# In image 0, three of sixteen units of x are loaded in 128-byte pieces and transposed by VectorE

## The chip, the cores and the metric

The kernel runs on one core of a Trainium2 chip. The metric is the device time of one execution in microseconds; "before" is the median of three runs. The engines named below are TensorE (PE; its weight loads are PEld), VectorE (DVE), ScalarE (ACT), GpSimd (POOL), and SyncE (SP), which here only issues transfers (DMAs). Transfers are carried by sixteen DMA engines.

## The reference

The input x is (4, 64, 64, 256) in float32: four images, each of N = 4096 positions with 256 channels. An attention layer is computed:

```python
q = x @ Wq + bq            # 128 channels per position
k = x @ Wk + bk            # 128 channels
v = x @ Wv + bv            # 256 channels
pq, pk, pv = (t.reshape(B, -1, N) for t in (q, k, v))
energy = einsum('bcn,bcm->bnm', pq, pk)
attention = softmax(energy, axis=-1)
out = einsum('bcm,bnm->bcn', pv, attention).reshape(B, W, H, C)
return gamma * out + x
```

The reshape is no transpose: it lays the position-by-channel block of an image out anew as channels by N. For the projections, x has to stand with its 256 channels on the partitions, so that TensorE can contract over them; in memory it lies with positions first. Somebody has to transpose it. The edit is about who.

## The kernel before

Products that need float32 accuracy are built from reduced-precision ones: a tensor y is split into forms h (upper part), l and d (combinations of y and h), and each product is taken as three matmuls over forms. ScalarE writes h, VectorE l, and d is written by VectorE or GpSimd (`split`, L153 to L168).

An image is projected in NI = 16 units of 256 positions each. Image 0 is projected first, in a loop of its own (its body begins with `products(0, i, 0, (0, 1))`), in about the first 64 us. Then comes the attention loop over 512 steps, in whose gaps the units of the next image are projected (`step`). Everything is scheduled by hand: each engine runs its instructions in the order in which the Python code issues them (`manual_schedule`), and semaphores are derived from the tiles that are written and read.

One pass of image 0's loop, for unit i, issues in this order:

- products of q and k with forms 0 and 1 of unit i (PE, L268); then `qk_forms` begins: ScalarE writes h of the tile f (L318);
- products of q and k with form 2 of unit i + 1 (PE), and then `seed_qk` (VectorE, L296), which puts the bias onto that result; the other products of unit i + 1, at the head of the next pass, accumulate onto it and so wait for it;
- VectorE's two other forms of f (L321). f holds q and k of unit i in all three forms and is stored to DRAM. Tiles f rotate over three buffers (two of the tag `pf`, and `f3`), so the L318 of unit i + 3 overwrites what unit i's stores read;
- products of v for unit i (PE); ScalarE's and VectorE's forms of v (L156, L159), GpSimd's third (L162); products of v with form 2 of unit i + 1, and `seed_v` (ScalarE, L303);
- `transposed(0, i + 3)`: four TensorE transposes of 128 x 128 into a PSUM tile `xt` (L230); then `x_forms(0, i + 3)`: ScalarE (L156), VectorE (L159), GpSimd (L162) split `xt` into the forms of x;
- `load_x(0, i + 6)`: SP loads a unit of x, 256 KB, into one of four slots `xs4` (L207). Each slot is read by the transposes of the unit before in it;
- `store()`: the stores of f, two of q and two of k for each unit, issued by SP (L349; for the units 0 to 3 one of them goes over GpSimd, L347);
- in the passes 7 to 14, parts of the first two attention steps (`cross` L379 and L380, `energy` L394 and L397, `upper` L403), and now and then a load of k by GpSimd (L366).

So SP's order in image 0 is: load of unit i + 6, stores of unit i, load of unit i + 7, stores of unit i + 1, and so on. Each of SP's transfers signals one of eight semaphores in turn, so that a ninth one waits until the first has landed.

For the images 1 to 3 the transpose is made in another way. There x is loaded by SP in eight transfers for a unit (L755), each of 32 KB in pieces of 128 bytes, so that every 32-channel group comes to lie on its own quarter of the partitions; a transpose of 32 x 32 blocks by VectorE (one instruction of 128 x 512, L226) then gives the same `xt` as TensorE's four transposes.

Of the kernel before, what the change touches and what calls it, by code (L numbers as in the profile page):

```python
# [20 lines left out]
def kernel(  # L21
# [36 lines left out]
    nc = tc.nc  # L58
# [5 lines left out]
    KC = C // P  # L64
# [5 lines left out]
    def columns(t, nb):  # L70
        return t.rearrange("b w h c -> b (w h c)").rearrange(
            "b (a s g f) -> b g a s f", a=P, s=2, f=nb
        )

    XB = 256
    xv = columns(x, XB)
# [24 lines left out]
    with ExitStack() as fast:  # L101
# [45 lines left out]
        active, stores, xloads = [], [], []  # L147
# [41 lines left out]
        def bank(name, shape, b, ring):  # L189
            if b:  # L190
                tile_ = spare(name, shape)
                now["turn"] += 1
                return tile_
            pool, tag = next(rings[ring])
            return pool.tile(shape, F32, tag=tag, name=name)

        def spare(name, shape):
            pool, tag = now["banks"][now["turn"] % len(now["banks"])]
            return pool.tile(shape, F32, tag=tag, name=name)

        def load_x(b, i):
            if b == B or i >= NI:
                return
            if b == 0:
                t = xs4[:, i % 4]
                if i:
                    nc.sync.dma_start(t, xv[b, i])  # L207
                loads["x", b, i] = t
                return
            pair = work.tile([P, 2, 2, XB], F32, tag="xd", name=f"x_{b}_{i}", bufs=1)  # L210
            for u in range(2):
                raw_x = pair[:, u].rearrange("p s f -> p (s f)")
                for q in range(4):
                    for k in range(KC):
                        to = raw_x[q * 32 : (q + 1) * 32, k * XB : (k + 1) * XB]
                        pieces = xv[b, i + u].rearrange(
                            "(c j) s (k q i) -> q k j s c i", j=32, k=KC, q=4
                        )
                        xloads.append((to.rearrange("j (s c i) -> j s c i", s=2, c=4), pieces[q, k]))
                loads["x", b, i + u] = raw_x  # L220

        def transposed(b, i):
            xs = loads.pop(("x", b, i))
            tp = units["xt", b, i] = bank(f"xt_{b}_{i}", [P, KC, 2, P], b, 0)
            if b:
                nc.vector.transpose(tp.rearrange("p k s a -> p (k s a)"), xs)  # L226
                return
            for k in range(KC):
                for s in range(2):
                    nc.tensor.transpose(tp[:, k, s, :], xs[:, s, k * P : (k + 1) * P], ident)  # L230
# [333 lines left out]
        def step(n, engine):  # L564
# [25 lines left out]
            elif engine == "act":  # L590
                if r in (3, 4):
                    begin(("x", r - 3), x_forms(b, i + r - 3))
                elif r in (7, 8):
                    begin(("qk", r - 7), qk_forms(b, i + r - 7))
                elif r in (10, 12):
                    seed_v_pair(b, i, r // 12)
                    if r == 12:
                        load_x(b + (i + 2) // NI, (i + 2) % NI)
                elif r in (11, 13):
                    begin(("v", r // 13), v_pair_forms(b, i, r // 13))  # L600
            else:
                if r in (1, 2):
                    transposed(b, i + r - 1)
                elif r in (3, 4):
                    next(made["x", r - 3])
                    next(made["x", r - 3])
                elif r == 5:
                    seed_qk(b, i)
                    seed_qk(b, i + 1)
                elif 7 <= r <= 10:  # L610
                    next(made["qk", (r - 7) // 2])
                    if r % 2 == 0:
                        next(made["qk", (r - 7) // 2], None)
                elif 11 <= r <= 14:
                    next(made["v", (r - 11) // 2])
                    if r % 2 == 0:
                        next(made["v", (r - 11) // 2], None)
# [7 lines left out]
        for i in range(4):  # L625
            load_x(0, i)
        transposed(0, 0)
        warm(2)
        w0, w1, x0 = weights(0), weights(1), x_forms(0, 0)
# [9 lines left out]
        products(0, 0, 0, (2,))  # L639
        seed_qk(0, 0)  # L640
        transposed(0, 1)
        warm(1)
        load_x(0, 4)
        x1 = x_forms(0, 1)
        next(x1)
# [54 lines left out]
        for n in range(B * STEPS):  # L700
            b, u = divmod(n, STEPS)
            g, t = divmod(u, NU)
# [13 lines left out]
            p = n - 2 + (n > 17)  # L716
# [32 lines left out]
            for m in range(2 * NU):  # L749
                c, r = divmod(n + NU - 3 - 13 * m // 16, STEPS)  # L750
# [11 lines left out]
    with tc.If(nc.values_load(again[0:1, 0:1]) > 0), ExitStack() as general:  # L762
# [91 lines left out]
        for b in range(B):  # L854
# [16 lines left out]
            for g in range(NG):  # L871
                ps = []
                mx = work.tile([P, 2, NB], F32, tag="mx", name=f"gmx_{b}_{g}")
                for t in range(NP):
# [9 lines left out]
                    p = ppool.tile([P, 2, NB], F32, tag="p", name=f"gp_{b}_{g}_{t}")  # L884
# [89 lines left out]
```

## Time and profile before

| | us |
|---|---|
| median of three runs | 2299.38 (2299.34 to 2299.46) |
| profiled execution | 2299.69 |
| its span in the trace | 2297.9 |
| TensorE busy | 2286.7 (100%) |
| VectorE busy | 2160.7 (94%) |
| ScalarE busy | 1794.1 (78%) |
| GpSimd busy | 445.0 (19%) |

Times in the views are microseconds from the start of the span. A row of a timeline has the start, the duration, the engine, the line, the operation with its tiles, the count of merged instructions, and in brackets the engine's idle time before it with what ended it. "SPq" marks an instruction by which SP issues a transfer; its duration is the issue, not the transfer. A row of a table by stretches has the stretch, its length, the busy time of PE, PEld, DVE, ACT and POOL (instructions in brackets), TensorE's granted clock as a share of full speed, the busy share of the DMA engines and GB/s. A row of a DMA queue has its packets, megabytes and the share of the sixteen engines' time. The names `qv`, `xf`, `xt`, `f` and `v` in the rows are the tiles named above.

### The profile page before, as it was taken

Reading aid. Unit: us, or ns where it says so; the run is one execution under the profiler, and the core shown is the slowest. Engines: PE = TensorE matmul, PEld = TensorE weight load, DVE = VectorE, ACT = ScalarE, POOL = GpSimd, SP = SyncE. Lnnn points to the kernel's source line nnn. Section 1 sums busy time; section 2 is a strip of 40 time slices with the busy share of each in tenths; the row PEclk is TensorE's granted clock in tenths of the full one; section 3 lists DMA queues with packets and bytes.
Section 4 is the critical chain, followed back from the end, with each engine's and each line's share of the span. In section 5 each row is a group of like instructions: output and inputs, shape, how many; then the busy total and the mean of one; then the engine's idle time right before and its main releaser. Section 6 shows DMA issues by size and latency. Waiting matters only on the chain.

```text
span 2297.9 us, 31904 instructions
## 1 busy us (share of the span) xinstructions
PE 2286.7 (100%) x10566; PEld 1911.9 (83%) x10566; DVE 2160.7 (94%) x2222; ACT 1794.1 (78%) x2917; POOL 445.0 (19%) x747
## 2 busy tenths in 40 slices
PE   9999999999999999999999999999999999999998
PEld 9888888888888888888888888888888888888886
DVE  8999999999999999999999999999999899888888
ACT  7778777787777877777777778777788777888885
POOL 7111111111231111111122111111112211111110
PEclk9999999999999999999999999999999999999999
DMA  8567766677996777666799667766689855555554
GB/s 272 161 171 212 196 179 165 174 211 194 279 278 195 195 195 193 178 170 183 208 293 287 179 178 207 199 177 170 169 227 300 243 149 144 135 137 147 151 142 107
DMA packets 305743, 445.31 MB, mean 194 GB/s; under 512 B 129698, under 2 KB 183204, under 8 KB 305572
## 3 DMA queue, kind: packets, MB, share of 16 engines
q0 software_dynamic: 105584, 296.79, 49.6%
q1 hardware_dynamic: 199568, 146.14, 20.8%
q8 instruction: 87, 1.43, 0.3%
q14 instruction: 84, 0.69, 0.1%
q10 hardware_dynamic: 420, 0.26, 0.0%
HBM read 313.79 MB, written 112.26 MB: 185 GB/s over the span
## 4 chain that ended last, share of the span: by engine, by line
PE 99%; DVE 0%; ACT 0%; DMA 0%; issue 0%; SPq 0%; DVEq 0%
PE a L453 40%; PE e L394 20%; PE b L453 20%; PE e L379 10%; PE qv L268 5%; PE v L285 3%; PE xt L230 0%; DMA xs<-in_x_dram 0%; ACT qv L303 0%; DVE ld L431 0%; PE zp L526 0%; DVE o_last L556 0%; DVE o_last L551 0%; DVE qv L296 0%; DVE o_last L557 0%
## 5 line engine op out<-in xcount | busy, mean ns | idle before, releaser
L397 ACT ACTIVATE x<-e 128x512 f32<-128x512 f32 x960 | 522.0, 596 | 324.1 <-PE e L394 324.1
L380 ACT ACTIVATE e<-e 128x512 f32<-128x512 f32 x1024 | 546.3, 571 | 114.9 <-PE e L379 114.9
L453 PE MATMUL a<-h,v 128*128 128x512 f32 x2048 | 631.3, 389 | 0.0
L453 PE MATMUL b<-ld,v 128*128 128x512 f32 x2048 | 631.0, 389 | 0.1
L453 PE MATMUL a<-ld,v 128*128 128x512 f32 x2048 | 630.9, 389 | 0.0
L414 DVE TENSOR_TENSOR s<-s,x 128x1024 f32<-128x1024 f32 x480 | 584.1, 1217 | 48.2 <-ACT x L397 46.7
L366 POOL DMA_DIRECT2D k<-kf x512 | 273.0, 533 | 1799.9 <-PE e L394 1750.0
L429 DVE TENSOR_TENSOR ld<-x,h 128x1024 fp32r<-128x1024 f32 x480 | 584.6, 1218 | 22.6 <-ACT h L403 22.2
L431 DVE SCALAR_TENSOR_TENSOR ld<-h,x 128x1024 fp32r<-128x1024 f32 x480 | 584.5, 1218 | 0.0
L394 PE MATMUL e<-q,k 128*128 128x512 f32 x2048 | 547.6, 389 | 0.0
L403 ACT ACTIVATE h<-x 128x1024 fp32r<-128x1024 f32 x480 | 510.7, 1064 | 14.2
L453 PEld LDWEIGHTS b<-ld,v 128*128 128x128 f32 x2048 | 384.1, 188 | 80.9 <-DVE ld L431 1.1
L453 PEld LDWEIGHTS a<-ld,v 128*128 128x128 f32 x2048 | 384.4, 188 | 80.4
L394 PEld LDWEIGHTS e<-q,k 128*128 128x128 f32 x2048 | 384.2, 188 | 79.8
L453 PEld LDWEIGHTS a<-h,v 128*128 128x128 f32 x2048 | 381.3, 188 | 76.0
L379 PE MATMUL e<-q,k 128*128 128x512 f32 x1024 | 315.4, 389 | 0.0
L379 PEld LDWEIGHTS e<-q,k 128*128 128x128 f32 x1024 | 192.0, 188 | 39.9
L321 DVE SCALAR_TENSOR_TENSOR f<-f,qv 128x512 fp32r<-128x512 f32 x128 | 85.7, 680 | 0.3
L268 PE MATMUL qv<-wf,xf 128*128 128x256 f32 x576 | 77.2, 285 | 0.5 <-DVE qv L296 0.2
L268 PEld LDWEIGHTS qv<-wf,xf 128*128 128x128 f32 x576 | 73.7, 191 | 3.7 <-DVE xf L166 0.6
L429 DVE TENSOR_TENSOR ld<-s,h 128x1024 fp32r<-128x1024 f32 x32 | 39.2, 1227 | 37.0 <-ACT h L403 34.3
L166 DVE SCALAR_TENSOR_TENSOR vf<-vf,v 128x512 fp32r<-128x512 f32 x96 | 65.3, 681 | 0.0
(87 smaller groups left out, 1098.5 us busy)
## 6 DMA issues: line engine op xcount, KB each, us to landing
k<-kf POOLq DMA_DIRECT2D x512, 384.0 KB, 3.8
vf<-vf SPq DMA_DIRECT2D x96, 384.0 KB, 4.8
v<-vf POOLq DMA_DIRECT2D x96, 384.0 KB, 6.1
kf<-f SPq DMA_DIRECT2D x128, 192.0 KB, 3.9
qd<-f SPq DMA_DIRECT2D x124, 192.0 KB, 4.0
q<-qd POOLq DMA_DIRECT2D x31, 768.0 KB, 4.9
o<-o POOLq DMA_DIRECT2D x31, 512.0 KB, 5.4
o<-in_x_dram POOLq DMA_DIRECT2D x31, 512.0 KB, 6.8
```

The source lines that it names most:

```text
L268: nc.tensor.matmul(to[:, s, :], left, right.rearrange("p s a -> p (s a)") if w else right, start=(f == 2 and s == k == 0), stop=(f == 1 an ...
L321: nc.vector.scalar_tensor_tensor(f[:, :, :, j, :], h.bitcast(F32), s, y, ALU.mult, op)
L366: nc.gpsimd.dma_start(t, kf[b, u % NU])
L379: nc.tensor.matmul(e, *forms(n, i, 2), start=True, stop=False, skip_group_check=True)
L380: nc.scalar.mul(e, e, -REST)
L394: nc.tensor.matmul(e, *forms(n, i, f), start=False, stop=(f == 1), skip_group_check=True)
L397: nc.scalar.activation(x[:, i, :], e, AF.Exp, scale=(1.0 + E) ** 3 / E)
L403: nc.scalar.activation(h, units[n], AF.Identity, scale=UPPER)
L414: nc.vector.tensor_tensor(s, s, x, ALU.add)
L429: nc.vector.tensor_tensor(l, x, h.bitcast(F32), ALU.subtract)
L431: nc.vector.scalar_tensor_tensor(d, h.bitcast(F32), 1.0 + E, x, ALU.mult, ALU.subtract)
L453: nc.tensor.matmul(to, vall[:, t, i, f, j * P : (j + 1) * P], units[n][f][:, i, :], start=(t == 0 and i == 0 and f != 1), stop=(t == NU - ...
```

## The change

For image 0, the units 8, 11 and 14 get what all units of the later images have: eight transfers in 128-byte pieces, issued by SP in the place of one, and one VectorE transpose in the place of four TensorE transposes. The other thirteen units stay as they were. The pieces' addresses move into a function of their own, which the later images use too, unchanged in what it does. The tile `xt`, its PSUM bank and all that reads it stay.

```diff
+        def x_pieces(t, b, i):
+            pieces = xv[b, i].rearrange("(c j) s (k q i) -> q k j s c i", j=32, k=KC, q=4)
+            for q in range(4):
+                for k in range(KC):
+                    to = t[q * 32 : (q + 1) * 32, k * XB : (k + 1) * XB]
+                    yield to.rearrange("j (s c i) -> j s c i", s=2, c=4), pieces[q, k]
+
+        BLOCKS = (8, 11, 14)
+
         def load_x(b, i):
             if b == B or i >= NI:
                 return
             if b == 0:
                 t = xs4[:, i % 4]
-                if i:
+                if i in BLOCKS:
+                    t = t.rearrange("p s f -> p (s f)")
+                    for to, pieces in x_pieces(t, b, i):
+                        nc.sync.dma_start(to, pieces)
+                elif i:
                     nc.sync.dma_start(t, xv[b, i])
                 loads["x", b, i] = t
                 return
...
             for u in range(2):
                 raw_x = pair[:, u].rearrange("p s f -> p (s f)")
...
+                xloads.extend(x_pieces(raw_x, b, i + u))
                 loads["x", b, i + u] = raw_x
 
         def transposed(b, i):
             xs = loads.pop(("x", b, i))
             tp = units["xt", b, i] = bank(f"xt_{b}_{i}", [P, KC, 2, P], b, 0)
-            if b:
+            if b or i in BLOCKS:
                 nc.vector.transpose(tp.rearrange("p k s a -> p (k s a)"), xs)
                 return
```

More of the change, by code (lines that the diff above doesn't have):

```diff
@@ L212, in load_x @@
                 raw_x = pair[:, u].rearrange("p s f -> p (s f)")
[L213 to L219, printed above, removed]
+                xloads.extend(x_pieces(raw_x, b, i + u))
                 loads["x", b, i + u] = raw_x
```

## The prediction

> **What bounds the kernel now.** I read the page first: engine shares, then the chain of work that ended last.
>
> ```profile
> span 2297.9 us, 31904 instructions
> PE 2286.7 (100%) x10566; PEld 1911.9 (83%) x10566; DVE 2160.7 (94%) x2222; ACT 1794.1 (78%) x2917; POOL 445.0 (19%) x747
> PE 99%; DVE 0%; ACT 0%; DMA 0%; issue 0%; SPq 0%; DVEq 0%
> ```
>
> TensorE is busy nearly throughout and holds 99% of the chain. So time taken from PE is won only if nothing else becomes late, and a microsecond of PE stall in image 0 is a microsecond at the end. The edit lies in image 0's projection stage (up to about 64 us), so I read three stretches there: each engine's busy time, the granted clock, the DMA share and GB/s.
>
> ```profile
> 25.30:28.60 3.30, 3.30 (x31) 3.30 (x30) 3.07 (x6) 2.44 (x5) 3.30 (x5) 1.00 0.96 311
> 32.00:35.30 3.30, 3.30 (x30) 3.30 (x29) 3.07 (x7) 2.44 (x5) 2.53 (x3) 1.00 1.08 379
> 46.20:49.50 3.30, 3.30 (x29) 3.22 (x28) 3.16 (x6) 3.27 (x7) 2.60 (x4) 1.00 0.67 236
> ```
>
> PE fills every 3.3 us; VectorE has 0.23 us free of 3.30, and the DMA engines are full until some time after 35 us. The clock is full, so it plays no part. Three resources have little to spare: PE, VectorE, and SP's queue with the DMA engines behind it.
>
> **TensorE: what is removed.** The timeline of PE at the transposes of units 8 and 9:
>
> ```profile
> 29.66 0.60 PE L230 MATMUL xt<-ident,xs 128*128 128x128 f32 x4
> 30.01 1.68 PE L268 MATMUL qv<-wf,xf 128*128 128x256 f32 x12
> 32.97 0.60 PE L230 MATMUL xt<-ident,xs 128*128 128x128 f32 x4
> 33.33 0.84 PE L268 MATMUL qv<-wf,xf 128*128 128x256 f32 x5
> ```
>
> Four transposes hold the next matmuls back by 30.01 - 29.66 = 0.35 us. Three units: -1.05 us, the most that can be won.
>
> **VectorE: what is added.** The same transpose runs for the later images. Its group, VectorE at units 8, 11 and 14, and the first product that needs the last seed:
>
> ```profile
> L226 DVE STREAM_TRANSPOSE xt<-x x48: 715/720/722, 82.2 to 1712.0; 128x512 f32<-128x512 f32 x48
> 30.43 0.68 DVE L159 SCALAR_TENSOR_TENSOR v<-v,qv 128x512 fp32r<-128x512 f32 x1
> 31.35 0.69 DVE L159 SCALAR_TENSOR_TENSOR xf<-xf,xt 128x512 fp32r<-128x512 f32 x1 [0.23 <-ACT xf L156]
> 31.95 0.69 DVE L296 SCALAR_TENSOR_TENSOR qv<-qv,bias 128x512 f32<-128x512 f32 x1
> ...
> 39.46 1.28 DVE L321 SCALAR_TENSOR_TENSOR f<-f,qv 128x512 fp32r<-128x512 f32 x2
> 40.66 0.68 DVE L159 SCALAR_TENSOR_TENSOR v<-v,qv 128x512 fp32r<-128x512 f32 x1
> 43.06 0.70 DVE L296 SCALAR_TENSOR_TENSOR qv<-qv,bias 128x512 f32<-128x512 f32 x1 [0.62 <-PE qv L268]
> ...
> 54.39 0.70 DVE L296 SCALAR_TENSOR_TENSOR qv<-qv,bias 128x512 f32<-128x512 f32 x1 [0.62 <-PE qv L268]
> ```
>
> ```profile
> 30.72 0.59 ACT L156 ACTIVATE xf<-xt 128x512 fp32r<-128x512 f32 x1
> 38.82 0.61 ACT L318 ACTIVATE f<-qv 128x512 fp32r<-128x512 f32 x1
> 50.14 0.61 ACT L318 ACTIVATE f<-qv 128x512 fp32r<-128x512 f32 x1
> ```
>
> ```profile
> 44.65 1.68 PE L268 MATMUL qv<-wf,xf 128*128 128x256 f32 x12
> 55.98 1.68 PE L268 MATMUL qv<-wf,xf 128*128 128x256 f32 x12
> ```
>
> The price is not only 0.72 us of VectorE: ScalarE's first form of x (0.59) must wait for the transpose, VectorE's form waits for ScalarE's, and behind that in VectorE's order stands the next seed (L296), which PE's next products need. Unit 8: the v form ends at 30.43 + 0.68 = 31.11; transpose to 31.83; ScalarE to 32.46 with 0.04 of hand-over (0.04 as in 30.72 + 0.59 to 31.35); VectorE's form from there, the seed 0.60 later (31.35 to 31.95), done at 33.75. PE without the four transposes wants it at 33.33 - 0.35 = 32.98 and restarts about 33.80: instead of winning 0.35 it is 0.47 later than before.
>
> At units 11 and 14 an energy step lies between, and VectorE waits 0.62 us for PE ahead of the seeds at 43.06 and 54.39. The same chain there gives a seed at 44.0 against PE's demand at 44.65 + 0.47 - 0.35 = 44.77: hidden, and the 0.35 won. By the engines alone the edit is 0.47 - 0.35 - 0.35 = -0.2 us.
>
> **SP's queue: what is added and moved past.** One 256 KB load becomes eight of 32 KB, three times; 21 more issues. Behind them on SP, in order, stand the stores of q and k and the next loads. SP's timeline, with image 1's sixteen such pieces for the price:
>
> ```profile
> 18.70 0.63 SPq L207 DMA_DIRECT2D xs<-in_x_dram  x1
> 20.64 0.80 SPq L349 DMA_DIRECT2D kf<-f  x2
> 22.03 0.57 SPq L207 DMA_DIRECT2D xs<-in_x_dram  x1
> 29.33 0.55 SPq L207 DMA_DIRECT2D xs<-in_x_dram  x1
> 30.57 0.32 SPq L349 DMA_DIRECT2D kf<-f  x1
> 32.06 0.68 SPq L349 DMA_DIRECT2D qd<-f  x1
> 33.89 0.52 SPq L349 DMA_DIRECT2D kf<-f  x1
> 36.06 0.55 SPq L207 DMA_DIRECT2D xs<-in_x_dram  x1
> 39.21 0.74 SPq L207 DMA_DIRECT2D xs<-in_x_dram  x1
> 68.20 10.55 SPq L755 DMA_DIRECT2D x<-in_x_dram  x16
> ```
>
> Sixteen pieces in 10.55 us is 0.66 each, so a unit holds SP for 5.28 us. Three stores hold it 1.4 us (20.64 to 22.03; so units 0 to 3), four 2.1 (33.89 to 36.06), the last issued 1.5 behind the first (30.57 to 32.06), a whole load 0.6. Played forward without a gap, since every store's data is ready earlier than its turn: unit 8's pieces 18.70 to 23.98; stores of unit 2 to 25.4, load 9 to 26.0, stores 3 to 27.5, load 10 to 28.1, stores 4 to 30.2; unit 11's pieces to 35.46; stores 5 from 35.46 (before: 30.57), the last issued at 36.96, SP free at 37.6; loads and stores of two more iterations to 42.96; unit 14's pieces to 48.24; the last of stores 8 at 49.74.
>
> Who waits: f has three buffers, so ScalarE's L318 for unit u+3 waits until the stores of unit u have landed. Unit 8's L318 is at 38.82, unit 11's at 50.14. From issue to landing the stores (L349) took, at about 21 and at about 31 us:
>
> ```profile
> DMA to landing us min/median/max: 2.1/2.7/2.7
> DMA to landing us min/median/max: 4.7/4.8/4.9
> ```
>
> I take 4.0, between the ends but nearer the loaded one, because the DMA engines are only partly drained while SP issues small pieces. Stores 5 land at 40.96; PE stands 0.47 later, so ScalarE wanted to write at 39.29 and is 1.7 late. From 40.96: ScalarE to 41.57, two f forms from 41.6 (1.20), v form to 43.48, transpose of unit 11 to 44.20, ScalarE and VectorE as above, seed done at 46.12 against 44.77: a stall of 1.35. PE then stands 0.47 - 0.35 + 1.35 = 1.47 late. Stores 8 land at 53.74; the write was wanted at 50.14 + 1.47 = 51.61; the same chain ends with the seed at 58.94 against 55.98 - 0.35 + 1.47 = 57.10: 1.84 of stall. The other units' stores come in time (unit 9's last issue at 52.4 lands at 56.4, wanted at 53.91 + 2.96).
>
> The sum: 0.47 - 0.35 + 1.35 - 0.35 + 1.84 = +2.96 us. With landings of 2.7 it is +1.7, with 5.0 it is +4.0.
>
> Costed at nothing: the landing of the pieces (unit 8's last issue by 24, first read at 31; unit 14's by 48.3, read after 56; cover gone only if SP is some 7 us later still); loads 12, 13 and 15, which have as much room; ScalarE's longer wait at the transpose, part of the chain above; after image 0 the work is the same, a later start moves it as a whole, and SP has drained its queue before image 1's pieces at 68.20.
>
> **The DMA engines.** The queue's share for the stretch of image 1's pieces (70 to 79 us) and for a stretch of mostly 1 KB packets (16 to 18.6 us):
>
> ```profile
> q1 hardware_dynamic: 3543, 0.43, 32.6%
> q1 hardware_dynamic: 533, 0.62, 73.4%
> ```
>
> 0.326 x 9 x 16 us over 3543 is 13 ns a packet, and 0.734 x 2.6 x 16 over 533 is 57 ns. A unit in pieces (2048 packets) takes 1.7 us of the sixteen engines, whole (256) 0.9. Since SP needs 5.28 us to issue it, the engines have time; added to the sum: nothing.
>
> The Trainium skill (DMA: Bandwidth & Descriptors, the opening table) holds that line rate needs at least 512 B, with a read-modify-write below. Then a piece would cost a 512 B packet, about half of 57 ns; the 13 ns here speak against it. What the sum would be by it is rival 3.
>
> **Against the measure.** The profiled run took 2299.69 us, 1.8 more than its span and 0.3 more than the median of 2299.38. The sum is a difference within that run and is put on the median: 2299.4 + 3.0 = 2302.4 us. A difference under 0.2% (4.6 us) is no change here.
>
> **Rivals.**
> 1. SP's lateness is covered after all (landings of 2.7 us and quicker issues): only the engine terms stay, -0.2, at best -1.05, at worst +0.8, 2298.3 to 2300.2. For it: the stores landed that fast at 20 us. Against: the 5.28 us of issue alone are more than an iteration.
> 2. Slower by over 0.2%: pieces issue slower than 0.66 us under a full DMA load. Every 0.01 us adds 24 x 0.01 = 0.24 us at stores 8, so from 0.73 it decides; at 0.80 the sum is +6.3, 2305.7 us. For it: the group of image 1's pieces reaches 2085 ns, and whole loads reach 737 at the time of full DMA; against: its median.
>
> ```profile
> L755 SPq DMA_DIRECT2D x<-in_x_dram x384: 578/611/2085, 68.2 to 1695.5; - x192
> L207 SPq DMA_DIRECT2D xs<-in_x_dram x5: 546/546/737, 29.3 to 43.4; - x5
> ```
>
> 3. A 128 B packet holds a DMA engine as long as half a 1 KB packet, 28 ns and not 13: 2048 x 28 / 16 is 3.6 us a unit, 1.9 more, and if both late stores land so much later, the sum is 3.0 + 3.8 = +6.8, 2306.2 us. Against it: the 13 ns counted above. The rule cited above would lead here.
> 4. The whole image stage is quicker and wins over 0.2%: PE's terms cannot give 4.6 us.
>
> **How the numbers follow.** Forecast (+1.2 to +4.4, that is 2300.6 to 2303.8): 0.64. Rival 1: 0.12. Rival 2: 0.21. Rival 3: 0.02. Rival 4: 0.01. Under 0.2% either way lie the forecast and rival 1: 0.76; slower: 0.23; faster: 0.01. The range leaves out half of rival 1 below and the far part of rivals 2 and 3 above: 2299.2 to 2305.8.
>
> **What would show it.** Right: SP issuing pieces at 0.66 us without a gap; stores of units 5 and 8 starting near 35.5 and 48.2; ScalarE idle before L318's successor at units 8 and 11, its releaser a DMA; PE idle before the products near 45 and 57, about 3 us in all, and image 0 ending some 3 us later. Wrong: L318 never waiting for a DMA (rival 1), a pitch above 0.73 (rival 2), a full DMA share while pieces flow (rival 3), or a difference that arises after 64 us.

## The result and the profile after

The changed kernel takes 2308.23 us (median of 6 runs, 2306.87 to 2311.72) beside 2299.47 us for the kernel before in the same comparison (6 runs, 2299.34 to 2301.96): a ratio of 1.004, 95% interval 1.0029 to 1.005. It is slower, by about 8.8 us. The prediction was +3.0 us. The profiled execution took 2307.9 us, 8.2 us more than that of the kernel before, and the readings below explain those 8.2 us. Every line number from L207 on is 7 to 13 higher than before: L325 is the write of `f` that was L318, L328 the two VectorE forms of `f` (L321), L356 the stores (L349), L275 the projections' products (L268).

The page of the kernel after: span, engines, and the chain of work that ended last.

```profile
span 2306.1 us, 31912 instructions
PE 2288.5 (99%) x10554; PEld 1912.8 (83%) x10554; DVE 2162.7 (94%) x2225; ACT 1794.4 (78%) x2917; POOL 445.3 (19%) x747
PE 98%; DMA 1%; ACT 0%; DVE 0%; SPq 0%; issue 0%; ACTq 0%; DVEq 0%
```

Twelve matmuls are gone and three VectorE transposes have come, as planned. What is new is "DMA 1%", where it was 0%: the chain now runs through transfers, on stores that land. SP's timeline after (start, duration of the issue, line, count) shows why:

```profile
18.71 5.36 SPq L218 DMA_DIRECT2D xs<-in_x_dram  x8
...
27.59 0.47 SPq L356 DMA_DIRECT2D qd<-f  x1
...
28.86 0.56 SPq L356 DMA_DIRECT2D kf<-f  x1
...
31.39 0.84 SPq L356 DMA_DIRECT2D qd<-f  x1
32.33 5.86 SPq L218 DMA_DIRECT2D xs<-in_x_dram  x8
38.30 0.54 SPq L356 DMA_DIRECT2D kf<-f  x1
...
39.85 0.47 SPq L356 DMA_DIRECT2D qd<-f  x1
...
46.95 5.29 SPq L218 DMA_DIRECT2D xs<-in_x_dram  x8
```

The eight pieces hold SP for 5.36, 5.86 and 5.29 us (0.67, 0.73 and 0.66 us each), and every store stands behind them: the stores of unit 5 begin at 38.30, where before they began at 30.57. It is the issuing that holds SP, and not the turn of the eight semaphores: between 18.71 and 58.0 us SP issues 59 transfers with 4.6 us between them in all, the two longest gaps being 0.54 and 0.44 us, and its waits for a landing sum to 0.9 us from 16 to 72 us. Who waits, in ScalarE's timeline (the bracket is the engine's idle time before the row and what ended it; the rows are the writes of `f` for units 6, 7 and 8):

```profile
33.71 0.60 ACT L325 ACTIVATE f<-qv 128x512 fp32r<-128x512 f32 x1 [1.61 <-DMA qd<-f]
...
37.18 0.60 ACT L325 ACTIVATE f<-qv 128x512 fp32r<-128x512 f32 x1 [1.04 <-DMA qd<-f]
...
45.04 0.60 ACT L325 ACTIVATE f<-qv 128x512 fp32r<-128x512 f32 x1 [4.46 <-DMA qd<-f]
```

Three writes of `f` wait for the stores that read the buffer three units ago. Unit 11's write, at 57.28, does not. The landing times of the transfers issued in three stretches, the stores of unit 4 (28.5 to 32 us), of unit 5 (38 to 40.2) and of unit 8 (52 to 55):

```profile
DMA to landing us min/median/max: 5.7/6.2/6.8
DMA to landing us min/median/max: 2.2/5.0/5.1
DMA to landing us min/median/max: 2.0/2.0/2.8
```

TensorE's timeline after, and behind it the row of the kernel before that answers to the last one:

```profile
33.49 1.21 PE L275 MATMUL qv<-wf,xf 128*128 128x256 f32 x8 [0.41 <-DVE qv L303]
35.78 0.71 PE L275 MATMUL qv<-wf,xf 128*128 128x256 f32 x4 [1.07 <-DVE f L328]
36.33 1.60 PE L275 MATMUL qv<-xf,wf 128*128 128x256 f32 x12
37.77 0.60 PE L237 MATMUL xt<-ident,xs 128*128 128x128 f32 x4
...
47.10 1.20 PE L275 MATMUL qv<-wf,xf 128*128 128x256 f32 x4 [3.51 <-DVE f L328]
48.09 2.76 PE L275 MATMUL qv<-xf,wf 128*128 128x256 f32 x12
50.65 1.06 PE L237 MATMUL xt<-ident,xs 128*128 128x128 f32 x4
...
53.31 1.60 PE L275 MATMUL qv<-xf,wf 128*128 128x256 f32 x12
...
64.67 0.72 PE L275 MATMUL qv<-wf,xf 128*128 128x256 f32 x4 [0.79 <-DVE f L328]
...
67.93 0.71 PE L275 MATMUL qv<-wf,xf 128*128 128x256 f32 x4 [0.15 <-DVE f L328]
...
72.17 0.63 PE L386 MATMUL e<-q,k 128*128 128x512 f32 x2
```

```profile
64.42 0.63 PE L379 MATMUL e<-q,k 128*128 128x512 f32 x2
```

The first energy step behind image 0's projections starts 72.17 - 64.42 = 7.75 us later, nearly all of the 8.2; what follows costs no more than it did. Two things make it up. First, PE stands still: 0.41 + 1.07 + 3.51 + 0.79 + 0.15 = 5.93 us. Second, behind the longest stop the same instructions take longer: twelve matmuls 2.76 us where the row at 36.33 has 1.60, four transposes 1.06 instead of 0.60. The stretches say why (PE, PEld, DVE, ACT and POOL busy with counts, granted TensorE clock, DMA share, GB/s):

```profile
22.00:25.30 3.30, 3.30 (x31) 3.30 (x30) 3.07 (x6) 2.44 (x5) 3.06 (x4) 1.00 0.63 128
35.30:38.60 3.30, 2.82 (x22) 2.81 (x23) 2.96 (x6) 2.26 (x5) 2.29 (x2) 1.00 0.43 78
42.40:46.20 3.80, 1.19 (x10) 0.94 (x8) 0.53 (x1) 1.16 (x3) 0.00 (x0) 0.91 1.05 379
46.20:49.50 3.30, 2.40 (x11) 2.43 (x12) 2.58 (x5) 1.93 (x5) 1.28 (x1) 0.50 0.95 325
49.50:53.00 3.50, 3.50 (x21) 3.50 (x20) 3.15 (x6) 3.41 (x7) 1.94 (x2) 0.59 0.36 59
```

The granted clock falls to 0.50. From the restart at 47.10 to 53.31 PE runs four matmuls, twelve, four transposes and twelve matmuls, in 6.21 us. At full speed these take, by the starts of rows, 0.55 (35.78 to 36.33), 1.44 (36.33 to 37.77), 0.35 (the transposes of before, 29.66 to 30.01) and 1.44 again, 3.78 in all: the lower clock costs 2.4 us. Not all of it is the clock's alone. The twelve behind the transposes need a seed that VectorE finished at 50.20 (it began at 49.51 and took 0.69), so by an estimate from these rows PE at full clock would have reached them at 49.44 and stood for some 0.8 us. So 5.9 of stops, 2.4 of half clock, less 1.05 for the transposes that PE no longer does, is 7.3; image 0 had to account for 8.1, since its first rows ran 0.34 earlier than before (the transposes of unit 4 at 16.07 and 16.41). The other 0.8 us lies in how a row counts idle time. It counts from the end of the last matmul, which is shown 0.28 us long, while in a dense row the next one starts 0.12 us behind it. Counted from start to start, the five stops cost 6.7 us and not 5.9, and 6.7 + 2.4 - 1.05 is 8.1.

The last two columns hold the third reading. While SP issues pieces the DMA engines are half empty (0.63 and 0.43, at 128 and 78 GB/s); behind them, when the held-back stores and loads come out together, they are full (1.05). This full stretch is where the stores of unit 5 land.

### The profile page after: what moved, and what is told of

The parts are those of the page before. It is cut to its first block, busy times and chain, and to the rows that moved or that the text cites. A ratio compares the mean times of both kernels' runs of the same rounds, so it can differ in the third digit from the quotient of the medians.

```text
span 2306.1 us, 31912 instructions
## 1 busy us (share of the span) xinstructions
PE 2288.5 (99%) x10554; PEld 1912.8 (83%) x10554; DVE 2162.7 (94%) x2225; ACT 1794.4 (78%) x2917; POOL 445.3 (19%) x747
## 4 chain that ended last, share of the span: by engine, by line
PE 98%; DMA 1%; ACT 0%; DVE 0%; SPq 0%; issue 0%; ACTq 0%; DVEq 0%
PE a L460 40%; PE b L460 20%; PE e L401 20%; PE e L386 10%; PE qv L275 4%; PE v L292 3%; DMA qd<-f 1%; SPq L356 0%; PE xt L237 0%; ACT qv L310 0%; ACT f L325 0%; DVE f L328 0%; ACT v L156 0%; DVE ld L438 0%; ACT h L410 0%
## 5 line engine op out<-in xcount | busy, mean ns | idle before, releaser
L328 DVE SCALAR_TENSOR_TENSOR f<-f,qv 128x512 fp32r<-128x512 f32 x128 | 85.7, 680 | 7.0 <-ACT f L325 6.5
L275 PE MATMUL qv<-wf,xf 128*128 128x256 f32 x576 | 79.0, 287 | 6.4 <-DVE f L328 5.5
L275 PEld LDWEIGHTS qv<-wf,xf 128*128 128x128 f32 x576 | 74.9, 193 | 10.5 <-issue 6.1
```

Of the source, the lines that this page charges most:

```text
L275: nc.tensor.matmul(to[:, s, :], left, right.rearrange("p s a -> p (s a)") if w else right, start=(f == 2 and s == k == 0), stop=(f == 1 an ...
L328: nc.vector.scalar_tensor_tensor(f[:, :, :, j, :], h.bitcast(F32), s, y, ALU.mult, op)
```

## Experiments

The theory after this reading, called S: what costs the time is the number of issues on SP, eight in the place of one; they hold back the stores, `f` becomes free late, and PE stops. Against it stand the new VectorE work, the 128-byte packets themselves, the buffers of `f` being too few, and the lower clock as a cost of its own. All edits are shown against the changed kernel unless said otherwise; each ratio is to the kernel before, in the same comparison. The ratios are those on record with their intervals; they are not the quotients of the two medians and differ from them by up to 0.05%.

**The VectorE transposes alone.** Units 8, 11 and 14 are loaded whole.

```diff
-                if i in BLOCKS:
-                    t = t.rearrange("p s f -> p (s f)")
-                    for to, pieces in x_pieces(t, b, i):
-                        nc.sync.dma_start(to, pieces)
-                elif i:
+                if i:
                     nc.sync.dma_start(t, xv[b, i])
```

> The three units are loaded whole as before, and VectorE transposes them; the 32 x 32 blocks stand in the wrong places, with all the work done. Theory (late stores behind the pieces): the loss is gone, -0.5 to +0.8 us against before, no wait of ScalarE's first form of f for a DMA; PE waits once, at unit 8's seed, by some 0.5 us. Rival (VectorE's chain): +4 us or more.

Measured: 2300.37 us beside 2299.61, +0.8 us, ratio 1.0003 (0.9994 to 1.0013). No write of `f` waits for a transfer. TensorE's timeline of this kernel:

```profile
33.57 1.99 PE L273 MATMUL qv<-wf,xf 128*128 128x256 f32 x12 [0.41 <-DVE qv L301]
```

The stop of 0.41 us at unit 8's seed is the only one above 0.2 us here, and the same that stands in the changed kernel at 33.49. The VectorE side is worth about what the interval can resolve. Even by the far ends of both intervals (6.7 us for the changed kernel, 3.0 here) 3.7 us come from the loads.

**The pieces alone.** The loads in pieces stay, TensorE transposes all sixteen units (the units' layout is then not that of the reference).

```diff
-            if b or i in BLOCKS:
+            if b:
```

> Units 8, 11 and 14 are loaded in pieces, but PE transposes them with its four transposes as before; the three units' channels stand in the wrong order, with all the work done. Theory (late stores behind the pieces): the whole loss of the changed kernel stays, +6.5 to +10 us against before. Rival (pieces cost only together with VectorE's transposes): within 2 us of before.

Measured: 2309.41 beside 2299.58, +9.8 us, ratio 1.004 (1.0025 to 1.0054). The waits of this kernel:

```profile
ACT f L324 <- DMA qd<-f: 11.6, 4, 4.9
```

The loads alone lose the whole time, as expected.

**Eight transfers without small packets.** The same three units in eight transfers each, but of sixteen partitions, so with rows of 1 KB: 32 packets a transfer in the place of 256 of 128 bytes. TensorE transposes them.

```diff
-                    t = t.rearrange("p s f -> p (s f)")
-                    for to, pieces in x_pieces(t, b, i):
-                        nc.sync.dma_start(to, pieces)
+                    for q in range(8):
+                        rows_ = slice(q * 16, (q + 1) * 16)
+                        nc.sync.dma_start(t[rows_], xv[b, i][rows_])
...
-            if b or i in BLOCKS:
+            if b:
```

> The kernel before, with the loads of units 8, 11 and 14 cut into eight transfers of 16 partitions with rows of 1 KB: as many issues of SP as in the changed kernel, but no 128-byte packets and PE's transposes. Theory A (it is the number of issues that holds SP: 21 more): SP's pitch is 0.5 us or more for these too, and the loss is +3 to +9 us. Theory B (the 128-byte packets hold the DMA engines or make each issue long): the pitch is 0.4 or less or the stores are soon through again, and the loss is under +2 us.

Measured: 2309.32 beside 2299.58, +9.7 us, ratio 1.0041 (1.0027 to 1.0055). SP's timeline, the waits and one stretch of this kernel:

```profile
19.20 5.12 SPq L218 DMA_DIRECT2D xs<-in_x_dram  x8
...
32.70 6.18 SPq L218 DMA_DIRECT2D xs<-in_x_dram  x8
...
47.40 5.78 SPq L218 DMA_DIRECT2D xs<-in_x_dram  x8
```

```profile
ACT f L325 <- DMA qd<-f: 11.7, 4, 3.9
```

```profile
35.30:38.90 3.60, 3.20 (x25) 3.14 (x26) 2.57 (x5) 1.87 (x5) 2.67 (x3) 1.00 0.22 64
```

This is the run that decides. With an eighth of the packets an issue holds SP as long (0.64, 0.77 and 0.72 us each), the wait for stores is as long as with pieces alone (11.7 and 11.6 us), and so is the loss, as far as intervals of some 3 us either way can tell. The packets' size is not the cause; with 1 KB rows the DMA engines are even emptier while the pieces are issued (0.22). What costs is the number of issues.

**More buffers for f.** The writes of `f` of units 3, 4, 5, 9 and 10 go to parts of `v`'s tile that are not yet written, so that fewer of them wait for a store.

```diff
+            if b == 0 and (3 <= i <= 5 or 9 <= i <= 10):
+                f = vall[:, NU - 1 - i % 3].rearrange("p s f (w a) -> p (s f w a)", w=2)
+                f = f.rearrange("p (s w f a) -> p s w f a", s=2, w=2, f=3)
-            if b == 0 and i % 3 == 2:
+            elif b == 0 and i % 3 == 2:
```

> The changed kernel, with the tiles f of units 3, 4, 5, 9 and 10 placed in slots of v that are not yet written, so that a store has about six passes of time and not three. Theory (the wait is for the f buffer): ScalarE's first form of f waits for no DMA, the stall of 3.5 us of PE and the clock drop behind it go, and the time is 0 to +3 us against before; what may be late next are the whole loads of x behind the pieces (unit 12's). Rival (the DMA engines as such are too busy, whichever buffer is used): +6 us or more.

Measured: 2309.05 beside 2299.61, +9.4 us, ratio 1.0036 (1.0022 to 1.005). I had overlooked that units 8 and 11 still share a buffer. Unit 8's wait is gone; the one write of `f` that waits for a store is unit 11's, by 5.7 us, and it stops PE instead. TensorE's timeline of this kernel:

```profile
59.32 0.87 PE L275 MATMUL qv<-wf,xf 128*128 128x256 f32 x4 [4.58 <-DVE f L331]
```

So a second version gives each late unit a buffer that no earlier unit holds (units 3 to 5 and 9, 10 in five parts of `v`, the rest in turn):

```diff
+            if b == 0 and i in (3, 4, 5, 9, 10):
+                f = vall[:, NU - 6 + i if i < 6 else NU - 11 + i].rearrange("p s f (w a) -> p (s f w a)", w=2)
+                f = f.rearrange("p (s w f a) -> p s w f a", s=2, w=2, f=3)
-            if b == 0 and i % 3 == 2:
+            elif b == 0 and i in (2, 8, 13):
```

> The changed kernel with f tiles of five units in slots of v not yet written, so arranged that a store has four to six passes of time up to unit 13 (in the run six_f units 8 and 11 still shared a buffer). Theory (the loss is ScalarE's wait for the stores of f): no such wait over 1 us, no clock drop, and +0.8 (VectorE's chain) to +3 us against before; what is left would be PE's wait for the late whole loads of x behind the pieces. Rival (SP and the DMA engines are short of time in sum, and what waits is only a matter of place): +5 us or more, with the wait at PE's transposes, at loads of k or at later stores.

Measured: 2307.09 beside 2299.58, +7.5 us, ratio 1.0031 (1.002 to 1.0041). The theory is missed, the rival met. The waits, TensorE's timeline and a stretch of this kernel:

```profile
ACT f L328 <- DMA qd<-f: 6.1, 2, 4.1
```

```profile
59.26 0.64 PE L237 MATMUL xt<-ident,xs 128*128 128x128 f32 x4 [1.86 <-issue]
...
69.78 1.22 PE L275 MATMUL qv<-xf,wf 128*128 128x256 f32 x8 [3.18 <-ACT qv L310]
```

```profile
69.70:71.00 1.30, 1.22 (x9) 1.22 (x10) 1.30 (x3) 0.03 (x1) 0.00 (x0) 1.00 1.07 392
```

The stops for `f` in the middle are gone, and two others have come. At 59.26 PE has stood 1.86 us ahead of transposes; the profile names no releaser, but the whole load that SP issued at 56.01, behind unit 14's pieces and unit 8's stores, landed at 59.16. And PE stands 3.18 us before 69.78, at a seed of ScalarE that comes behind a late write of `f`: at the end of image 0 a write has waited 4.1 us for a store again. (In this execution image 0 also began 1.7 us later than in that of the changed kernel: unit 8's first piece is issued at 20.43 and not 18.71.) SP issues from 20.43 us to the end of image 0 almost without a gap. From the load of unit 8 on, the kernel before issues 56 transfers that hold SP 28.8 us out of 45.9; with 21 more it is 77 that hold it 43.7 us in the changed kernel and 43.9 here, nearly all of the 45.9 that this part took before. SP has no slack left to work lateness off. More buffers move the place where this is paid; they do not pay it.

**The pieces spread out.** On the same buffers, the pieces are issued three, three and two behind the stores of three passes (shown against that version).

```diff
+        later = []
...
-                    for to, pieces in x_pieces(t, b, i):
-                        nc.sync.dma_start(to, pieces)
+                    later.extend(x_pieces(t, b, i))
...
+            for to, pieces in later[:3]:
+                nc.sync.dma_start(to, pieces)
+            del later[:3]
```

> As deep_f, but the pieces of a unit are issued 3, 3 and 2 in three passes, behind each pass's stores, in the place of eight in a row ahead of them. Theory: no load or store of x or f is later than its slack, +0.5 to +1.5 us against before. Rival (SP and the DMA engines are short in sum): no better than deep_f, +4 us or more.

Measured: 2314.41 beside 2299.58, +14.8 us, ratio 1.0061 (1.0044 to 1.0078). The waits of this kernel:

```profile
DVE xt L233 <- DMA xs<-in_x_dram: 12.1, 3, 6.2
```

Now the stores go first and the x tiles themselves come too late: VectorE waits 12.1 us for them. That is the rival's case: spreading takes nothing from the sum on SP.

**The pieces off SP.** The pieces are issued by ScalarE and GpSimd, two each in two passes.

```diff
+        later = []
...
-                    for to, pieces in x_pieces(t, b, i):
-                        nc.sync.dma_start(to, pieces)
+                    later.extend(x_pieces(t, b, i))
...
+            for m, (to, pieces) in enumerate(later[:4]):
+                (nc.scalar, nc.gpsimd)[m % 2].dma_start(to, pieces)
+            del later[:4]
```

> The changed kernel, with the 24 pieces issued by ScalarE and GpSimd (two each in the passes u - 6 and u - 5 of a unit u, behind what they do in the pass) and none by SP. The DMA engines carry the same 128-byte packets. Theory (SP's time to issue is what is short): the stores of f are in time, no wait of ScalarE's first form for them, and the time is +0.5 to +3 us against before (VectorE's chain, and what the issues take of ScalarE and GpSimd). Rival (the packets on the DMA engines): +5 us or more with waits for stores as in the changed kernel.

Measured: 2307.41 beside 2299.51, +7.9 us, ratio 1.0032 (1.002 to 1.0044). The expectation is missed. The waits of this kernel, and from the timelines of GpSimd and of ScalarE's issues:

```profile
PEld qv L275 <- POOL xf L162: 2.7, 3, 1.9
...
DVE xt L233 <- DMA xs<-in_x_dram: 2.5, 1, 2.5
...
ACT s L404 <- DMA kf<-f: 2.0, 1, 2.0
...
ACT f L325 <- DMA kf<-f: 1.2, 1, 1.2
```

```profile
24.14 1.29 POOL L696 DMA_DIRECT2D xs<-in_x_dram  x2
```

```profile
47.13 2.52 ACTq L696 DMA_DIRECT2D xs<-in_x_dram  x2
```

What S says of `f` holds: of 7.1 us of waiting for stores 1.2 are left. But the issues cost elsewhere. One takes about 0.65 us on GpSimd (1.29 for two), and GpSimd writes forms of x that PE needs; PE's weight loads wait for it three times. VectorE waits 2.5 us for a piece. And the longest stop of PE, 2.44 us before 52.74, leads back to ScalarE: of the 2.52 us in the last row two issues take 0.59 each, and in between ScalarE stands until a store of k that SP had issued has landed (the 2.0 us in the waits), for its transfers and SP's signal the same eight semaphores in turn; behind this its write of `f` comes at 50.67. The run moves the cost and doesn't take it away, so it does not separate the issues from their queue. With units 11 and 14 alone handled so (unit 8 as before):

> As off_sp, with the units 11 and 14 alone, whose VectorE chain was worked out to be hidden. If both chains are hidden and the issues find room on ScalarE and GpSimd, PE gains 2 x 0.35 us: -0.7 to 0 against before. If the issues delay ScalarE's or GpSimd's forms: 0 to +2.

2305.63 beside 2299.51, +6.1 us, ratio 1.0024 (1.0014 to 1.0034): missed as well. Its longest stop is 2.10 us before 48.34, again at `f`'s forms.

**One unit at a time.** `BLOCKS` is cut to unit 8, and to unit 14.

```diff
-        BLOCKS = (8, 11, 14)
+        BLOCKS = (8,)
```

> The changed kernel with unit 8 alone in pieces. Theory (SP's issues pile up from unit to unit and the piled-up lateness meets the f buffers): the lateness of one unit is worked off in three passes, the time is +0.5 to +2.5 us against before, and the three units cost more together than three times one. Rival (each unit has its own price): +2.5 to +3.5.

Measured: 2303.46 (2300.91 to 2306.8) beside 2299.51, +4.0 us by the medians and 3.0 by the ratio, 1.0013 (1.0004 to 1.0023); more than expected. The profiled execution was the longest of the ten, 2306.8 us; image 0 began late in it, unit 8's first piece being issued at 20.98 and not 18.71, that is, ahead of the first transfer that the edit touches. TensorE's timeline and a stretch of it:

```profile
38.53 1.19 PE L275 MATMUL qv<-wf,xf 128*128 128x256 f32 x4 [2.09 <-DVE f L328]
```

```profile
38.50:41.00 2.50, 2.47 (x11) 2.50 (x12) 2.35 (x5) 0.99 (x2) 1.94 (x2) 0.50 0.94 321
```

A stop of 2.09 us, and then half clock. The late write of `f` ahead of this stop waited for the stores of unit 3, which stood behind the pieces: the profile names a product of PE as its releaser, but the last of these stores, issued at 29.83, landed 6.5 us later, at 36.36, and the write began at 36.47. Whether such a stop halves the clock, and how late image 0 begins, may be what spreads these ten runs over 5.9 us, where those of before lie within 2.5; only one of them has a trace, so this is not shown.

> The changed kernel with unit 14 alone in pieces. Theory (piled-up lateness): -0.35 to +2 us against before; the stores of unit 8 land about 1 us late for unit 11's first form. Rival (each unit has its own price): +2.5 to +3.5.

Unit 14 alone: 2300.8 (2299.38 to 2304.09) beside 2299.51, +1.3 us, ratio 1.0005 (0.9996 to 1.0014). Its longest stop is at unit 11's `f`, by the stores of unit 8 behind the pieces; one of 0.58 us at the seed follows (57.97). TensorE's timeline:

```profile
54.80 0.71 PE L275 MATMUL qv<-wf,xf 128*128 128x256 f32 x4 [1.63 <-DVE f L328]
```

That is where the prediction had put a stall of 1.84 us, in a kernel without the other two units. That the sizes are so near is in part luck: the prediction had PE 1.47 us late by then, and here one of unit 8's stores held SP 1.92 us. Nor do the two runs show lateness piling up: three times 4.0 would be more than the 8.8 of three units, and unit 14's interval (-0.9 to +3.2 us) reaches into the rival's range. With the buffers of the second version above:

> Unit 14 alone in pieces, with the f tiles of deep_f, so that the stores of unit 8, late behind the pieces, hold nobody in unit 11. Theory (late stores are the price, VectorE's chain at unit 14 is hidden): the stall of 1.6 us of the run only_14 goes, and PE wins its four transposes, -0.4 to +0.4 us against before. Rival (SP's lateness only moves, to the loads or the later stores): +1 us or more, as only_14.

2299.94 beside 2299.46, +0.5 us, ratio 1.0000 (0.9991 to 1.001). No write of `f` waits for a store, and TensorE's timeline has the first energy step behind the projections where it stood before (64.42):

```profile
64.39 0.63 PE L389 MATMUL e<-q,k 128*128 128x512 f32 x2
```

One unit's seven extra issues were hidden by more buffers, three units' were not. Nothing is won either; no version was faster than the kernel before.

**The clock.** Does the half clock cost its 2.4 us beside the stop? In the longest stop, the pass of unit 9, PE gets 28 matmuls with weights of zero that add nothing to a bank.

```diff
+            if i == 5:
+                zero_r = vall[:, NU - 1, 0, 0, :P]
+                nc.gpsimd.tensor_scalar(zero_r, ones, 0.0, None, ALU.mult)
+            if i == 9:
+                for m in range(28):
+                    nc.tensor.matmul(
+                        units[0, 0, 9][:, m % 2, :], zero_r, wf[:, 0, 0, 0],
+                        start=False, stop=(m > 25), skip_group_check=True,
+                    )
```

> The changed kernel, with 28 products of zero weights (about 3.3 us) added to the sums of unit 9 at the place where PE stood idle for 3.5 us; they add nothing to the result. If the granted clock of 0.5 from 47 to 52 us comes from that idle time, it stays at full and the time is 2 to 3 us less than the changed kernel's, about +6 against before. Rival (the clock falls for another cause, or what PE loses at half clock is hidden behind VectorE and ScalarE): the same as the changed kernel or slower, +8 to +12.

Measured: 2308.82 beside 2299.61, +9.2 us, ratio 1.0039 (1.0024 to 1.0053). A stretch, and TensorE's timeline:

```profile
44.00:48.00 4.00, 4.00 (x36) 4.00 (x35) 2.52 (x4) 2.49 (x6) 1.26 (x1) 1.00 1.07 395
```

```profile
43.39 3.52 PE L666 MATMUL qv<-wf,v 128*128 128x256 f32 x28
...
61.33 0.98 PE L275 MATMUL qv<-wf,xf 128*128 128x256 f32 x3 [2.60 <-DVE f L328]
```

With PE busy the clock stays at 1.00 in the place where it had fallen to 0.50: the idle stretch is what lowers it. But the time does not come back. PE comes earlier to the pass of unit 12, and there stands 2.60 us for unit 11's `f`, which in the changed kernel came in time. The same fill at unit 12 as well:

> As filled_gap, with 28 products of zero weights also in the pass of unit 12, where PE stood idle for 2.6 us in that run and the granted clock fell behind it. Theory C (the half clock after an idle stretch of PE adds its own time to the stall): no stretch at half clock in image 0, and 2 to 3 us less than the changed kernel, about +6 against before. Theory S (SP's issues set the pace of the stage; PE at full clock only comes earlier to the next wait): the clock stays full, and the time is within 1.5 us of the changed kernel's, +7.5 to +10 against before.

2309.4 beside 2299.46, +9.9 us, ratio 1.0044 (1.0028 to 1.0059), with the clock full in all of image 0; but here the second fill itself holds PE some 3 us. That is in theory S's range. What the half clock costs by itself stays open. What is shown is that PE's pace was not the limit: taking the 2.4 us away let PE run into the next late store.

## Why the prediction was wrong

Its mechanism was right in kind: SP's issues hold back the stores, `f` becomes free late, and PE stops. The sum gave +3.0, the runs +8.8. It forecast 4.0 us of stops (0.82, 1.35 and 1.84) less 1.05; image 0 shows 6.7 us of stops less 1.05, and 2.4 us of half clock. The steps that failed are SP's time to issue under load, the landing time, the two units whose stores were not tested, and the clock.

- **TensorE, -1.05 us.** Twelve matmuls went, and nothing speaks against 0.35 us a unit; it can't be seen by itself in the end time.
- **VectorE's chain.** Right: PE at unit 8's seed was forecast to restart 0.47 us late, at 33.80; measured 33.49 with image 0 running 0.34 us ahead, so 33.83. Behind the late write of unit 8 the chain also has the forecast length: from the write at 45.04 to the end of the seed at 50.20 is 5.16 us, as from 40.96 to 46.12. But PE stopped ahead of it, at the products that wait for the forms of `f` (L328). At unit 11 and 14 no seed stopped PE. The engine terms were -0.2 us; the run with transposes alone has +0.8 and does not contradict it (interval about -1.4 to +3.0).
- **SP played forward.** This is the term that failed most. The order and the first unit were right (24.07 against 23.98), the rest too quick. The stores of unit 5 were put at 35.46 and came at 38.30. Of these 2.84 us, 0.76 were there when unit 4's stores began (28.86 against 28.1); those four and the gap behind them took 3.47 us against 2.1; unit 11's pieces took 5.97 against 5.28. All prices had been taken from rows where SP had idle time or the DMA engines did. With both full some issues were longer: the last three stores of unit 4 took 0.93, 0.90 and 0.84 us, at a DMA share of 1.10, and one piece of unit 11 took 1.02.
- **Landing 4.0 us.** Unit 5's last store, issued at 39.85, set ScalarE free at 45.04, 5.2 us later. The prediction's 4.0 stood between 2.7 and 4.8 on the ground that small pieces drain the DMA engines. They do drain (0.43), but the stores are issued behind the pieces, together with everything else that was held back, into a share of 1.05. With issue and landing, ScalarE's write for unit 8 was ready at 45.04 and not 40.96, and the stop was 3.51 and not 1.35 us: of these 4.08 us 2.89 are SP's (39.85 against 36.96) and 1.19 the landing's.
- **"The other units' stores come in time."** Wrong for units 3 and 4. Unit 3's last store was issued at 27.59, half a microsecond later than forecast (SP was to be through with it at 27.5 and was at 28.06), but ScalarE could write only at 33.71, 6.1 us later, where it was wanted at 32.10: 1.61 us, and 1.07 of them on PE. A landing of 4.0 would have been in time. The prediction had tested one unit only, unit 9, whose stores come behind the last pieces.
- **Unit 11, a stall of 1.84.** It did not occur in the changed kernel, since PE came there so much later and unit 8's stores landed in 2.0 to 2.8 us. With unit 14 alone it did occur, with 1.63.
- **"The clock is full, so it plays no part."** The clock is full before; that a stop would lower it was left out. It ran at half for some 5 us behind the 3.51 us stop, 2.4 us by the rows, though the filled runs leave open how much of that the next store would have taken anyway. Image 0 has no such stop in the profile before, so nothing there could price this; a chance for it could have been given.
- **The DMA engines, nothing.** Right for the pieces: the 1 KB version loses as much, and rival 3 falls with it, although its 2306.2 us lies nearer to the result than the forecast. The Trainium skill's rule on 512 B (DMA: Bandwidth & Descriptors, the opening table) would have led there. A byte in small packets does hold the engines about twice as long by the prediction's rows (1.7 us a unit against 0.9), but the 1 KB version shows that this is not what the kernel pays for. Wrong for the stores behind the pieces, as said.
- **Rival 2.** Its condition was half met, 0.73 us at unit 11 and 0.67 and 0.66 at the others; by its own price (0.24 us for each 0.01 above 0.66, at a mean of 0.69) it gives 0.7 us and not 5.8. It named the right resource with too small a consequence.
- **Slips.** Stores 3 end at 27.4 by the prediction's own terms, not 27.5, and the last seed at 58.90, not 58.94; neither changes the forecast.

## What to carry to other kernels

Count what a stage asks of each queue that issues transfers, as for an engine, before splitting a transfer: here seven more issues a unit at 0.66 us and more were more than a 3.3 us pass had free, whatever the size of their packets, and the bill came at a buffer that a late store still held. Take the landing time from the most loaded row, test every store in the delayed stretch and not only the first, and don't expect more buffers to help where the queue is short in sum. If the sum contains a stop of PE of 2 us or more, add a case in which the clock falls behind it.

## What the runs showed of the hardware

- **Issuing costs by the transfer, not by its packets.** Eight issues of 32 packets of 1 KB took 5.12 to 6.18 us, eight of 256 packets of 128 B 5.29 to 5.86; a whole load of 256 KB held SP 0.55 to 0.63 in the kernel before. On GpSimd an issue took about 0.65.
- **A landing under full load takes 4.7 to 6.8 us,** against 2.0 to 2.8 when the DMA engines have room, for stores of `f` alike: 4.7 to 4.9 in the kernel before at a share of 1.08, 5.7 to 6.8 for unit 4's in the changed kernel at 1.10, 2.0 to 2.8 for unit 8's there.
- **Stops well under 3 us can halve TensorE's clock.** 0.50 was granted behind stops of 3.51 us (the changed kernel), 2.60 (the filled one) and 2.09 (unit 8 alone), but not behind 1.63 (unit 14 alone), nor behind 3.18 us in the version with more buffers, whose stretch above keeps 1.00. So length alone does not decide. The half-speed stretches last about 3.4 or 6.8 us in the records. The Trainium skill (TensorE: Matmul & The Clock Gate, Part 1) tells of a free-running window of 3413 ns and of half rate after at least one idle window. The steps of 3.4 us and the dependence on more than the length agree with a free-running window; that stops of 2.09 and 2.60 us, shorter than a window, were enough does not agree with a whole idle one. Its section "Why this matters for your kernels" asks that gaps of more than about 3 us be avoided; here one of 2.09 us was enough.
